# Order of the first seven steps in a four-layer graph attention kernel: a one-head step in third place

## The chip, the cores and the metric

The kernel runs on one core of a Trainium2 chip. The metric is the time of one execution on the device in microseconds (us), lower is better. A core has five engines that each work through a queue of their own: TensorE (PE in the profile; PEld is its loading of weights), VectorE (DVE), ScalarE (ACT), GpSimd (POOL), and SyncE (SP), which here only issues DMAs.

## The reference

Sixteen batches of 1024 nodes with 256 features go through four graph attention layers, one after the other, with a residual connection. The mask is one 1024x1024 adjacency matrix. Per layer:

```
h = relu(layernorm(x))
q = h @ W                              # per head: 4 heads of 64, or 1 head of 256
e = leaky_relu(q @ a_src + (q @ a_dst).T)      # 1024 x 1024 per head
p = softmax(where(adj > 0, e, -inf))
x = x + elu(p @ q)                     # relu in the last layer
```

Layers 0 and 2 have four heads, layers 1 and 3 have one. All arithmetic is in 32-bit floats.

## The kernel before

A *step* is one layer of one batch: 64 steps, `(batch, layer)`. Four batches are in flight at a time (streams 0 to 3), and `order_of_steps` gives the order in which their steps are taken, as a list of streams in `turns`. A step needs the step before it of the same stream to be finished.

A step has three phases.

- *Preparation* (`preparation`, a list of 21 pieces). `stats` takes bn_stats on VectorE, `combine` and `combine_end` make scale and shift of them (on GpSimd; on VectorE, with only the power on GpSimd, in step 0 and in the last step). `normalise` writes relu of the normalised rows on ScalarE. `transpose` turns them: in steps 0, 1 and the last by TensorE, with a copy on ScalarE; elsewhere by `split` (ScalarE), a DMA transpose (SP queue) and `merge` (ScalarE). `project` multiplies by the layer's weights on TensorE, its result `whx` is copied by ScalarE and scaled by GpSimd. `factors` and `rows` make the row factors, which go out to memory (`grow`) and come back broadcast over all partitions (`fetch`, tile `gs`), to be copied to PSUM by `broadcast` (tile `g`, two buffers). In step 0's first head and in the last step (`direct`) TensorE broadcasts instead.
- *Weights and aggregation*. `weights` makes one tile of attention weights, 128 x 1024, by one VectorE instruction (L455): the larger of row factor and column factor, times the mask. A four-head step has 32 such tiles, a one-head step 8. They have 18 buffers. `aggregate` sums them over `whx` on TensorE (L472): eight groups for a four-head step (`h`, `i0`), eight row blocks for a one-head step; ScalarE copies each group's result to `y` (L487).
- *Finishing* (`finish`): the division by the sum (`divide`), the elu (its exponential on ScalarE, L525) and the residual addition, on VectorE and GpSimd. In the third step from the end the finishing is done on VectorE as a chain of its own (`early`, `late`, `begin`, `end`), with the last step's statistics in it, since that step follows in the same stream with only one other step between.

The order within an engine is the order in which the Python code emits (`manual_schedule`). The main loop goes over steps and groups `k`: it aggregates a group, emits what finishing has at `k`, then the preparation pieces due, then further weight tiles, up to 6 (four heads) or 3 (one head) more. When a preparation piece is due is told by tables of 21 times in units of a group, eight to a step: `kind` chooses a table for a step and `start` the group from which it counts. Step 1 uses `FIRST`, step 2 uses `SOON`, the last one `LAST`. `slack(n)` says that the next step has one head.

Of the kernel before, what the change touches and what calls it, by code (L numbers as in the profile page):

```python
# [32 lines left out]
ALU = mybir.AluOpType  # L33
# [14 lines left out]

FOUR = (-8, -8, -5, 0, 1, 0, 3, 5, 5, 5, 5, 1, 4, 5, 5, 5, 5, 6, 8, 8, 10)
SHORT = (-4, -4, -4, 0, 1, 0, 3, 5, 5, 5, 5, 1, 4, 5, 5, 5, 5, 6, 8, 8, 10)
NEXT = (-4, -4, -4, 1, 3, 2, 5, 8, 8, 8, 8, 4, 7, 8, 8, 8, 8, 9, 10, 10, 12)
ONE = (2, 2, 2, 3, 4, 3, 5, 7, 7, 7, 7, 4, 7, 8, 8, 8, 8, 8, 11, 11, 12)
SOON = (0, 0, 0, 1, 2, 1, 3, 4, 4, 5, 5, 2, 5, 6, 6, 7, 7, 7, 8, 8, 10)
FIRST = (-4, -4, -4, -2, -0.9, -1, -1, -0.8, -0.8, -0.8, -0.8, 0, 0, 1, 1, 1, 1, 1, 2, 2, 4)
TIGHT = (4, 4, 4, 5, 6, 5, 7, 8, 8, 8, 8, 6, 8, 9, 9, 9, 9, 9, 10, 10, 12)
LAST = (0, 0, 0, 1, 3, 2.8, 2.8, 4, 4, 4, 4, 4, 4, 4, 4, 4, 4, 4, 5, 5, 5)
LATE = (0, 0, 0, 1, 2, 1, 3, 4, 4, 4, 4, 2, 4, 5, 5, 5, 5, 5, 6, 6, 8)


LAYERS = [
    (4, 0.2, 0, 0),
    (1, 0.2, 0, 0),
    (4, 0.2, 128, 1),
    (1, 0.01, 0, 1),
]
# [3 lines left out]
def kernel(ctx: ExitStack, tc: tile.TileContext, x, adj, ws, avs, out):  # L71
    nc = tc.nc
# [37 lines left out]

    L = len(LAYERS)
    steps = order_of_steps(B, L)
    xs = {}
    state = [dict() for _ in steps]

    def bank(*shape):
        t = ps.tile([P, 512], F32, name="bank")
        n = math.prod(shape)
        if len(shape) == 1:
            return t[:, 0:n]  # L120
        names = "abc"[:len(shape)]
        return t[:, 0:n].rearrange(f"p ({' '.join(names)}) -> p {' '.join(names)}",
                                   **dict(zip(names, shape)))
# [151 lines left out]
    def preparation(n):  # L275

        b, l = steps[n]
# [4 lines left out]
        def stats(half):  # L282
            if half == 0:
                st["bn"] = small.tile([P, C, 6], F32, name="bn")
            bn = st["bn"]
            for c in range(half * HALF, (half + 1) * HALF):
                nc.vector.bn_stats(bn[:, c, :], xs[b][:, c, :])  # L287
            q = slice(half * HALF, (half + 1) * HALF)
            if n == len(steps) - 1:
                combine(q, nc.vector)  # L290
            elif n == 0:
                if half == 1:
                    combine_end(slice(0, HALF), nc.vector)
                combine(q, nc.vector)
            elif H == 1:

                combine(q, nc.gpsimd)
                combine_end(q, nc.gpsimd)
# [26 lines left out]
        def combine_end(q, engine):  # L325
            rstd, shift = (st[i][:, q] for i in ("rstd", "shift"))
            engine.tensor_tensor(shift, shift, rstd, op=ALU.mult)
            engine.tensor_scalar(shift, shift, -0.5, None, op0=ALU.mult)  # L328
# [25 lines left out]
                st["turned", half].rearrange("p s n i -> p (n i) s"), AF.Copy)  # L354

        def transpose(half, k):
            if 1 < n < len(steps) - 1:

                (merge if k else split)(half)
                return  # L360
            if k == 0:
                st["hT", half] = prep.tile([P, K, HALF * P], F32, name="rows", bufs=HBUFS)
            pt = bank(HALF, P)
            for q in range(HALF):
                nc.tensor.transpose(pt[:, q, :], st["xn", half][:, k, q, :], ident)
            nc.scalar.activation(st["hT", half][:, k, :], pt.rearrange("p q i -> p (q i)"),
                                 AF.Copy)
# [28 lines left out]

        def rows():

            if n == len(steps) - 1:
                return  # L400
            pt = bank(P)[0:C * H]
            nc.tensor.transpose(pt, st["gcol"].rearrange("p c h -> p (c h)"), ident)  # L402
            gT = small.tile([C * H, P], F32, name="gT", bufs=2)
            nc.scalar.activation(gT, pt, AF.Copy)
            st["grow"] = dram.tile([H, C, P], F32, name="grow")
            nc.sync.dma_start(out=st["grow"].rearrange("h c i -> c h i"), in_=gT)
# [5 lines left out]


        out += [factors, rows, lambda: fetch_heads(n + 1), lambda: None]
        if n == len(steps) - 1:
            st["stats"], st["combined"] = stats, lambda half: combine_end(
                slice(half * HALF, (half + 1) * HALF), nc.vector)
            out[0:3] = [lambda: None] * 3
        return [(at, piece) for at, piece in zip(agenda_of[n], out, strict=True)]

    def direct(n, h):

        return h == 0 and n in (0, len(steps) - 1)

    def fetch(n, h):

# [16 lines left out]
    def weights(n, h, jc):  # L443


        parts = 2 if n == len(steps) - 1 else 1
        if parts > 1 and jc:
            return
        js = range(C) if parts > 1 else (jc,)
        for j in js:  # L450
            state[n]["w", h, j] = work.tile([P, N], F32, name="w", bufs=WBUFS)
        for i in range(parts):
            s = slice(i * N // parts, (i + 1) * N // parts)
            for j in js:
                nc.vector.scalar_tensor_tensor(  # L455
                    state[n]["w", h, j][:, s], state[n]["g", h][:, s],
                    state[n]["rcol"][:, j, h:h + 1],
                    masks[LAYERS[steps[n][1]][3]][:, j, s], op0=ALU.max, op1=ALU.mult)
# [30 lines left out]
    def slack(n):  # L489

        return LAYERS[steps[n + 1][1]][0] == 1

    def finish(n):

        b, l = steps[n]
# [27 lines left out]
        def exponential(half):  # L523
            if l < L - 1:
                nc.scalar.activation(st["e", half], st["e", half], AF.Exp)  # L525
# [19 lines left out]
            if half == 1 and b + STREAMS < B:  # L545
                load(b + STREAMS)

        if n == len(steps) - 3:

            def early(half):  # L550
                xh, yh, r = views(half)
                rb = r[:, :, None].to_broadcast([P, HALF * H, D])
                e = st["e", half] = prep.tile([P, HALF * H, D], F32, name="rows", bufs=HBUFS)
                nc.vector.scalar_tensor_tensor(e, yh, 0.0, rb, op0=ALU.min, op1=ALU.mult)  # L554
                if half == 0:
                    exponential(half)
                nc.vector.tensor_tensor(yh, yh, rb, op=ALU.mult)

            def late(half):
                xh, yh, r = views(half)  # L560
                e = st["e", half]
                nc.vector.scalar_tensor_tensor(e, e, -1.0, yh, op0=ALU.add, op1=ALU.max)
                nc.vector.tensor_add(xh, xh, e)

            def begin():
                divide()
                early(0)
                late(0)
                state[-1]["stats"](0)
                early(1)  # L570
                state[-1]["combined"](0)

            def end():
                late(1)
                state[-1]["stats"](1)
                state[-1]["combined"](1)

            return [(-1, begin), (1, lambda: exponential(1)), (1, end)]


        at = (0, 0, 0, 0, 1, 1, 1) if slack(n) and H > 1 else (0, 0, 1, 1, 2, 2, 3)
# [31 lines left out]
    def fetch_heads(below=0):  # L613

        done["rows"] = max(done["rows"], below)
        while done["gs"] < min(done["g"] + 2 * C, len(tiles)):
            n, h, _ = tiles[done["gs"]]
            if n >= done["rows"]:
                break
            fetch(n, h)  # L620
            done["gs"] += C
# [23 lines left out]
    for n, (b, l) in enumerate(steps):  # L645

        free = -99
        if b % STREAMS in last:
            over = last[b % STREAMS] + 1
            free = 8 * over + (8 if l == 0 else 2 if LAYERS[steps[over][1]][0] == 1 else 4)  # L650
        last[b % STREAMS] = n
        start = 8 * (n - 2)
        kind = ONE if LAYERS[l][0] == 1 else SOON if n < 3 else FOUR
        if kind is FOUR and free > start + kind[0]:
            kind = SHORT if slack(n - 2) else NEXT
        if kind is ONE and free > start + kind[0]:
            kind = TIGHT
        if free > start + kind[0]:
            kind = LATE
            start = max(free, agenda_of[-1][0] + 5, start - LATE[7])  # L660
        if n == len(steps) - 1:
            kind, start = LAST, 8 * (n - 1)
        agenda_of.append([start + k for k in kind] if n > 1 else FIRST)
        if n > 2:


            assert agenda_of[n][7] >= 8 * (n - 2)
            assert agenda_of[n][3] >= agenda_of[n - 1][12]
# [76 lines left out]
def order_of_steps(B, L):  # L745

    depth = B // STREAMS * L  # L750
    one = [[(k // L * STREAMS + s, k % L) for k in range(depth)] for s in range(STREAMS)]
    turns = [0, 1, 2, 0, 3, 1, 2] + [0, 3, 1, 0, 2, 1, 3, 2] * (depth // 2 - 1) + [3]
    return [one[s].pop(0) for s in turns]


# [22 lines left out]
```

## Time and profile before

| | us |
|---|---|
| median of 3 runs | 2445.25 |
| their range | 2444.63 to 2452.23 |
| profiled execution, its own time | 2449.74 |
| its span from first to last instruction | 2448.0 |
| busy: TensorE | 2394.8 (98%) |
| busy: VectorE | 2040.0 (83%) |
| busy: ScalarE | 1480.0 (60%) |
| busy: GpSimd | 1073.7 (44%) |

The profile is of one execution. A group of it collects the instructions of one line and form; behind the busy time stands the time that the engine was idle just before them, and what ended it. A timeline lists start, duration, engine, line, operation and count, with such idle time in brackets. Matmuls are pipelined, so a busy TensorE need not be at its peak.

Where the first seven steps end in this execution (by the last aggregation): step 1 at about 135 us, the third step, (2,0), at 180, and the seventh, (2,1), at 327.3.

### The profile page before, as it was taken

The numbers are of one execution on the slowest core, as the hardware profiler recorded it, in microseconds if no ns is written. First come the engines' busy times: TensorE is split into PE (matmuls) and PEld (weight loads), VectorE is DVE, ScalarE is ACT, GpSimd is POOL, SyncE is SP. The second block draws the span as 40 slices with busy tenths as digits, with TensorE's granted clock in tenths as the row PEclk, the third lists the DMA queues.
The fourth block names the chain that finished last, engine by engine and source line by source line (L and its number), as shares of the span: only waits on it lengthen the run. The fifth ranks groups of instructions, "written<-read, shape, count | busy, mean of one in ns | idle before, by whom it ended". The sixth has DMA issues, their size and how long they took to land.

```text
span 2448.0 us, 86681 instructions
## 1 busy us (share of the span) xinstructions
PE 2394.8 (98%) x39177; PEld 2153.2 (88%) x39177; DVE 2040.0 (83%) x2141; ACT 1480.0 (60%) x2505; POOL 1073.7 (44%) x1350
## 2 busy tenths in 40 slices
PE   7999999999999999999999999999999999999999
PEld 5888899899888888898998888888988998988987
DVE  8988588898888988887988888888889888888794
ACT  5465676565666656765656765566655577656542
POOL 3345455433345454544433554543443345545331
PEclk9999999999999999999999999999999999999999
DMA  5322233243333222323433322224334323223220
GB/s 182 83 53 63 45 79 67 66 114 92 85 96 79 72 63 52 74 71 96 114 89 88 80 62 71 64 50 108 75 93 114 95 48 80 68 65 76 75 54 35
DMA packets 292220, 191.84 MB, mean 78 GB/s; under 512 B 261778, under 2 KB 264586, under 8 KB 289930
## 3 DMA queue, kind: packets, MB, share of 16 engines
q1 hardware_dynamic: 291840, 186.29, 30.6%
q8 instruction: 307, 5.03, 0.9%
q14 instruction: 63, 0.52, 0.1%
q10 hardware_dynamic: 10, 0.00, 0.0%
HBM read 104.87 MB, written 17.43 MB: 50 GB/s over the span
## 4 chain that ended last, share of the span: by engine, by line
PE 82%; ACT 7%; DMA 5%; DVE 4%; issue 2%; POOL 0%; SPq 0%; DVEq 0%; ACTq 0%
PE bank L472 64%; PE bank L376 17%; DVE w L455 2%; DMA gs<-grow 2%; ACT rows L334 2%; DMA grow<-gT 2%; ACT g L441 1%; ACT rows L343 1%; ACT rows L525 1%; ACT rows L351 1%; ACT y L487 1%; DVE bn L287 1%; DMA rows<-rows 0%; PE bank L402 0%; ACT whx L378 0%
## 5 line engine op out<-in xcount | busy, mean ns | idle before, releaser
L472 PE MATMUL bank<-whx,w 128*64 128x65 f32 x36864 | 1898.0, 240 | 17.9 <-DVE w L455 9.3
L472 PEld LDWEIGHTS bank<-whx,w 128*64 128x64 f32 x36864 | 1745.7, 144 | 173.9 <-ACT whx L378 21.8
L455 DVE SCALAR_TENSOR_TENSOR w<-g,rcol,mask 128x1024 f32<-128x1024 f32 (+1 forms) x1288 | 1540.2, 1270 | 204.0 <-PE bank L472 165.2
L388 POOL TENSOR_TENSOR whx<-whx 128x1024 f32<-128x1024 f32 x128 | 244.5, 1910 | 819.1 <-ACT whx L386 819.1
L487 ACT ACTIVATE y<-bank 128x260 f32<-128x260 f32 (+1 forms) x504 | 192.1, 381 | 567.7 <-PE bank L472 567.7
L376 PE MATMUL bank<-wx,rows 128*128 128x264 f32 (+1 forms) x2048 | 484.8, 390 | 15.4 <-ACT y L487 11.8
L376 PEld LDWEIGHTS bank<-wx,rows 128*128 128x128 f32 x2048 | 380.9, 190 | 90.9 <-ACT y L487 17.9
L519 POOL TENSOR_TENSOR y<-y,r 128x1024 f32<-128x1024 f32 x124 | 259.0, 2098 | 222.0 <-DVE rows L518 188.4
L334 ACT ACTIVATE rows<-x,shift,rstd 128x256 f32<-128x256 f32 x512 | 265.2, 591 | 66.7 <-POOL shift L328 62.2
L378 ACT ACTIVATE whx<-bank 128x264 f32<-128x264 f32 (+1 forms) x512 | 193.7, 388 | 184.9 <-PE bank L376 184.6
L532 POOL TENSOR_TENSOR x<-x,rows 128x1024 f32<-128x1024 f32 x94 | 222.4, 2365 | 177.9 <-DVE rows L531 177.9
L351 ACT ACTIVATE rows<-rows 128x2048 uint16<-128x2048 uint16 x122 | 261.6, 2144 | 22.7 <-DMA rows<-rows 22.6
L343 ACT ACTIVATE rows<-rows 128x2048 uint16<-128x2048 uint16 x122 | 233.3, 1912 | 3.9
L531 DVE SCALAR_TENSOR_TENSOR rows<-rows,y 128x1024 f32<-128x1024 f32 x94 | 186.6, 1986 | 42.8 <-ACT rows L525 39.1
L287 DVE BATCH_NORM_STATS2 bn<-x 128x6 f32<-128x256 f32 x512 | 175.8, 412 | 34.5 <-POOL x L532 31.1
L441 ACT ACTIVATE g<-gs 128x1024 f32<-128x1024 f32 x158 | 161.8, 1024 | 67.1 <-DMA gs<-grow 55.9
L322 POOL TENSOR_TENSOR rstd<-rstd,neghalf 128x4 f32<-128x4 f32 (+1 forms) x97 | 121.3, 1251 | 41.1 <-DVE shift L323 33.8
L525 ACT ACTIVATE rows<-rows 128x1024 f32<-128x1024 f32 x96 | 100.7, 1048 | 4.2 <-DVE rows L554 4.2
L508 DVE RECIPROCAL r<-y 128x32 f32<-128x32 f32 (+1 forms) x63 | 17.4, 277 | 100.9 <-ACT y L487 100.9
L518 DVE SCALAR_TENSOR_TENSOR rows<-y,r 128x1024 f32<-128x1024 f32 x58 | 70.2, 1251 | 1.1
L386 ACT ACTIVATE whx<-whx,nbias 128x16 f32<-128x16 f32 (+1 forms) x128 | 40.4, 316 | 4.2
L384 ACT ACTIVATE rcol<-whx,rbias 128x16 f32<-128x16 f32 (+1 forms) x128 | 40.0, 313 | 4.2
(82 smaller groups left out, 461.9 us busy)
## 6 DMA issues: line engine op xcount, KB each, us to landing
gs<-grow SPq DMA_DIRECT2D x158, 512.0 KB
x<-in_x SPq DMA_DIRECT2D x15, 1024.0 KB
out<-x SPq DMA_DIRECT2D x30, 512.0 KB
w<-in_adj SPq DMA_DIRECT2D x8, 512.0 KB
rows<-rows SPq DMA_TRANSPOSE x122
x<-in_x SPq DMA_DIRECT2D x2, 512.0 KB
wx<-in_L_gnn_W SPq DMA_DIRECT2D x8, 128.0 KB
out<-x SPq DMA_DIRECT2D x8, 128.0 KB
```

The source lines that it names most:

```text
L287: nc.vector.bn_stats(bn[:, c, :], xs[b][:, c, :])
L334: nc.scalar.activation(xn[:, :, q, :], xs[b][:, c, :].rearrange("p (k i) -> p k i", k=K), AF.Relu, bias=st["shift"][:, c:c + 1], scale=st[ ...
L343: nc.scalar.activation(bits, xn.rearrange("p (n s) -> p s n", s=2), AF.Copy)
L351: nc.scalar.activation(st["hT", half].rearrange("p k i -> p (k i)").bitcast(U16).rearrange("p (n s) -> p n s", s=2), st["turned", half].re ...
L376: nc.tensor.matmul(pw, lhsT=st["hT", half][:, k, q * P:(q + 1) * P], rhs=wx[l][:, k, :], start=(k == 0), stop=(k == K - 1))
L378: nc.scalar.activation(st["whx"][:, c, :], pw, AF.Copy)
L388: nc.gpsimd.tensor_tensor(wh[:, :, :, 0:D], wh[:, :, :, 0:D], wh[:, :, :, D:D + 1].to_broadcast([P, HALF, H, D]), op=ALU.mult)
L455: nc.vector.scalar_tensor_tensor(state[n]["w", h, j][:, s], state[n]["g", h][:, s], state[n]["rcol"][:, j, h:h + 1], masks[LAYERS[steps[n] ...
L472: nc.tensor.matmul(acc[o % P:o % P + cols, q, :], lhsT=st["w", h, jc][:, o:o + cols], rhs=st["whx"][:, jc, h * (D + 1):(h + 1) * (D + 1)], ...
L487: nc.scalar.activation(st["y"][:, i0:i0 + per, h, :], acc, AF.Copy)
L519: nc.gpsimd.tensor_tensor(yh, yh, rb, op=ALU.mult)
L532: nc.gpsimd.tensor_add(xh, xh, e)
```

## The change

In the list of turns the third step becomes stream 0's one-head layer 1, and the two four-head steps of streams 2 and 3 come fourth and sixth:

```
before: (0,0) (1,0) (2,0) (0,1) (3,0) (1,1) (2,1) ...
after:  (0,0) (1,0) (0,1) (2,0) (1,1) (3,0) (2,1) ...
```

From the seventh step on the order is as before. The third step (n = 2) is treated as the last step is (`rush`): statistics combined on VectorE, transposes on TensorE, `direct` broadcast of its row factors, weights in halves; its preparation is placed by a new table `THIRD`, within step 1. Step 0 is finished by the chain on VectorE, save one multiplication on GpSimd; the chain is cut into `begin`, `middle` and `end`, `middle` and `end` at group 1 of step 1. The fourth step (n = 3) gets a new table `FOURTH`, counted from group 8 (the start of step 1), so its statistics come after group 4 of step 0 and its projections at the end of step 0 and after step 1's first group. `SOON` goes.

```diff
 FOUR = (-8, -8, -5, 0, 1, 0, 3, 5, 5, 5, 5, 1, 4, 5, 5, 5, 5, 6, 8, 8, 10)
 SHORT = (-4, -4, -4, 0, 1, 0, 3, 5, 5, 5, 5, 1, 4, 5, 5, 5, 5, 6, 8, 8, 10)
 NEXT = (-4, -4, -4, 1, 3, 2, 5, 8, 8, 8, 8, 4, 7, 8, 8, 8, 8, 9, 10, 10, 12)
 ONE = (2, 2, 2, 3, 4, 3, 5, 7, 7, 7, 7, 4, 7, 8, 8, 8, 8, 8, 11, 11, 12)
-SOON = (0, 0, 0, 1, 2, 1, 3, 4, 4, 5, 5, 2, 5, 6, 6, 7, 7, 7, 8, 8, 10)
 FIRST = (-4, -4, -4, -2, -0.9, -1, -1, -0.8, -0.8, -0.8, -0.8, 0, 0, 1, 1, 1, 1, 1, 2, 2, 4)
 TIGHT = (4, 4, 4, 5, 6, 5, 7, 8, 8, 8, 8, 6, 8, 9, 9, 9, 9, 9, 10, 10, 12)
+THIRD = (1, 1, 1, 1, 3, 1.8, 1.8, 1.9, 1.9, 1.9, 1.9, 3, 3, 3, 3, 3, 3, 3, 5, 5, 5)
+FOURTH = (-4, -4, -4, -3, -2, -3, -1, -1, -1, -1, -1, -2, 0, 0, 0, 0, 0, 0, 0, 0, 7)
 LAST = (0, 0, 0, 1, 3, 2.8, 2.8, 4, 4, 4, 4, 4, 4, 4, 4, 4, 4, 4, 5, 5, 5)
 LATE = (0, 0, 0, 1, 2, 1, 3, 4, 4, 4, 4, 2, 4, 5, 5, 5, 5, 5, 6, 6, 8)
...
     steps = order_of_steps(B, L)
     xs = {}
     state = [dict() for _ in steps]
+    rush = (2, len(steps) - 1)
     def bank(*shape):
         t = ps.tile([P, 512], F32, name="bank")
...
             for c in range(half * HALF, (half + 1) * HALF):
                 nc.vector.bn_stats(bn[:, c, :], xs[b][:, c, :])
             q = slice(half * HALF, (half + 1) * HALF)
-            if n == len(steps) - 1:
+            if n in rush:
                 combine(q, nc.vector)
             elif n == 0:
                 if half == 1:
...
                 st["turned", half].rearrange("p s n i -> p (n i) s"), AF.Copy)
         def transpose(half, k):
-            if 1 < n < len(steps) - 1:
+            if n > 1 and n not in rush:
                 (merge if k else split)(half)
                 return
...
         def rows():
-            if n == len(steps) - 1:
+            if n in rush:
                 return
             pt = bank(P)[0:C * H]
             nc.tensor.transpose(pt, st["gcol"].rearrange("p c h -> p (c h)"), ident)
...
         out += [factors, rows, lambda: fetch_heads(n + 1), lambda: None]
-        if n == len(steps) - 1:
+        if n in rush:
             st["stats"], st["combined"] = stats, lambda half: combine_end(
                 slice(half * HALF, (half + 1) * HALF), nc.vector)
             out[0:3] = [lambda: None] * 3
...
     def direct(n, h):
-        return h == 0 and n in (0, len(steps) - 1)
+        return h == 0 and (n == 0 or n in rush)
     def fetch(n, h):
...
     def weights(n, h, jc):
-        parts = 2 if n == len(steps) - 1 else 1
+        parts = 2 if n in rush else 1
         if parts > 1 and jc:
             return
         js = range(C) if parts > 1 else (jc,)
...
             if half == 1 and b + STREAMS < B:
                 load(b + STREAMS)
-        if n == len(steps) - 3:
+        if n + 2 in rush:
+            after = state[n + 2]
             def early(half):
                 xh, yh, r = views(half)
                 rb = r[:, :, None].to_broadcast([P, HALF * H, D])
                 e = st["e", half] = prep.tile([P, HALF * H, D], F32, name="rows", bufs=HBUFS)
                 nc.vector.scalar_tensor_tensor(e, yh, 0.0, rb, op0=ALU.min, op1=ALU.mult)
-                if half == 0:
-                    exponential(half)
-                nc.vector.tensor_tensor(yh, yh, rb, op=ALU.mult)
+                (nc.vector if n else nc.gpsimd).tensor_tensor(yh, yh, rb, op=ALU.mult)
             def late(half):
                 xh, yh, r = views(half)
...
             def begin():
                 divide()
                 early(0)
+            def middle():
+                exponential(0)
                 late(0)
-                state[-1]["stats"](0)
+                after["stats"](0)
                 early(1)
-                state[-1]["combined"](0)
+                after["combined"](0)
             def end():
+                exponential(1)
                 late(1)
-                state[-1]["stats"](1)
-                state[-1]["combined"](1)
-
-            return [(-1, begin), (1, lambda: exponential(1)), (1, end)]
+                after["stats"](1)
+                after["combined"](1)
+            return [(-1, begin), (-1 if n else 1, middle), (1, end)]
         at = (0, 0, 0, 0, 1, 1, 1) if slack(n) and H > 1 else (0, 0, 1, 1, 2, 2, 3)
...
             free = 8 * over + (8 if l == 0 else 2 if LAYERS[steps[over][1]][0] == 1 else 4)
         last[b % STREAMS] = n
         start = 8 * (n - 2)
-        kind = ONE if LAYERS[l][0] == 1 else SOON if n < 3 else FOUR
+        kind = ONE if LAYERS[l][0] == 1 else FOUR
         if kind is FOUR and free > start + kind[0]:
             kind = SHORT if slack(n - 2) else NEXT
         if kind is ONE and free > start + kind[0]:
...
         if free > start + kind[0]:
             kind = LATE
             start = max(free, agenda_of[-1][0] + 5, start - LATE[7])
-        if n == len(steps) - 1:
-            kind, start = LAST, 8 * (n - 1)
+        if n == 3:
+            kind, start = FOURTH, 8
+        if n in rush:
+            kind, start = THIRD if n == 2 else LAST, 8 * (n - 1)
         agenda_of.append([start + k for k in kind] if n > 1 else FIRST)
-        if n > 2:
+        if n > 3:
             assert agenda_of[n][7] >= 8 * (n - 2)
...
     depth = B // STREAMS * L
     one = [[(k // L * STREAMS + s, k % L) for k in range(depth)] for s in range(STREAMS)]
-    turns = [0, 1, 2, 0, 3, 1, 2] + [0, 3, 1, 0, 2, 1, 3, 2] * (depth // 2 - 1) + [3]
+    turns = [0, 1, 0, 2, 1, 3, 2] + [0, 3, 1, 0, 2, 1, 3, 2] * (depth // 2 - 1) + [3]
     return [one[s].pop(0) for s in turns]
```

## The prediction

> **What bounds the kernel now.** I read the page first, then the timelines of VectorE, TensorE and ScalarE up to 345 us, because the diff moves work only there. All later steps keep their order.
>
> From the page (share of the span; then count | busy us, mean ns | idle before):
>
> ```profile
> PE 2394.8 (98%) x39177; PEld 2153.2 (88%) x39177; DVE 2040.0 (83%) x2141; ACT 1480.0 (60%) x2505; POOL 1073.7 (44%) x1350
> ...
> L472 PE MATMUL bank<-whx,w 128*64 128x65 f32 x36864 | 1898.0, 240 | 17.9 <-DVE w L455 9.3
> ...
> L455 DVE SCALAR_TENSOR_TENSOR w<-g,rcol,mask 128x1024 f32<-128x1024 f32 (+1 forms) x1288 | 1540.2, 1270 | 204.0 <-PE bank L472 165.2
> ...
> L334 ACT ACTIVATE rows<-x,shift,rstd 128x256 f32<-128x256 f32 x512 | 265.2, 591 | 66.7 <-POOL shift L328 62.2
> ...
> L351 ACT ACTIVATE rows<-rows 128x2048 uint16<-128x2048 uint16 x122 | 261.6, 2144 | 22.7 <-DMA rows<-rows 22.6
> L343 ACT ACTIVATE rows<-rows 128x2048 uint16<-128x2048 uint16 x122 | 233.3, 1912 | 3.9
> ```
>
> TensorE is busy nearly all the time; a group of a four-head step takes 3.79 us back to back (the timeline has three in 11.36), a row block of a one-head step 3.53 us (three in 10.59), a projection 7.35 us. So a four-head step needs 8 x 3.79 + 7.35 + 0.27 = 38 us of TensorE, a one-head step 8 x 3.53 + 7.35 + 0.27 = 36. VectorE needs 32 weight instructions for a four-head step and 8 for a one-head step, at a pitch of 1.194 us (47.75 / 40 below): 38.2 us, and about 9 us of finishing and statistics on top, against 9.6 and some 6. A four-head step is thus bound by VectorE, a one-head step by TensorE. The start has three four-head steps in a row. VectorE's timeline (start us, us, engine, line, out<-in, count):
>
> ```profile
> 47.87 47.75 DVE L455 SCALAR_TENSOR_TENSOR w<-g,rcol,mask 128x1024 f32<-128x1024 f32 x40
> 95.53 0.35 DVE L508 RECIPROCAL r<-y 128x32 f32<-128x32 f32 x1
> ...
> 98.35 2.48 DVE L455 SCALAR_TENSOR_TENSOR w<-g,rcol,mask 128x1024 f32<-128x1024 f32 x2
> ...
> 107.94 1.23 DVE L531 SCALAR_TENSOR_TENSOR rows<-rows,y 128x1024 f32<-128x1024 f32 x1
> ...
> 112.64 7.23 DVE L455 SCALAR_TENSOR_TENSOR w<-g,rcol,mask 128x1024 f32<-128x1024 f32 x6
> ...
> 122.40 19.15 DVE L455 SCALAR_TENSOR_TENSOR w<-g,rcol,mask 128x1024 f32<-128x1024 f32 x16
> ```
>
> It runs without a hole, so it is the bound there. TensorE's timeline shows the price:
>
> ```profile
> 116.35 0.34 PE L472 MATMUL bank<-whx,w 128*64 128x65 f32 x4 [0.66 <-DVE w L455]
> 117.54 0.34 PE L472 MATMUL bank<-whx,w 128*64 128x65 f32 x4 [0.85 <-DVE w L455]
> ...
> 183.72 14.07 PE L472 MATMUL bank<-whx,w 128*128 128x257 f32 x64
> ```
>
> From 108 to 135 us TensorE takes four matmuls per weight tile and waits for the next (releaser L455). The last row is step 3's one-head work: four blocks in 14.07, without a wait. From 44.4 us (first aggregation) to 327.3 (end of the seventh step) TensorE's work is 32 x 3.79 + 24 x 3.53 + 3.65 + 6 x 7.35 + set-up of layers 1 to 3 (8.1) + rows (1.9) + transposes (1.1) = 265 us in 283: **18 us are lost there**, all that a better order could win.
>
> **What the Trainium skill says.** "Perfetto Trace Analysis", section Sequencer Loop: an engine instruction waits for its semaphores in its engine's queue, read in program order; so an instruction held up holds all behind it. The trace agrees: a group that TensorE ended at 143.99 us had its y copied at 147.07 only, behind a normalise and a split on ScalarE, and TensorE waited 0.70 us for that copy. "TensorE: Matmul & The Clock Gate", section What's actually happening: after an idle window of some 3.4 us the array runs at half clock for about as long. The trace agrees (PE, PEld, DVE, ACT, POOL busy, then clock granted):
>
> ```profile
> 33.00:36.70 3.70, 0.04 (x1) 0.00 (x0) 3.59 (x4) 3.32 (x5) 0.00 (x0) 0.76 0.27 82
> 36.70:39.60 2.90, 2.75 (x8) 1.48 (x8) 2.90 (x4) 2.88 (x7) 0.00 (x0) 0.50 0.74 263
> ```
>
> After 3.7 idle us the clock is 0.50, and the next 16 projection matmuls take 4.87 us in place of 3.75: 1.1 us for such a hole.
>
> **The change, part by part.** Following the planner's loop gives each engine's new order; the durations are those of before.
>
> *Order.* Stream 0's layer 1 becomes step 2, (2,0) step 3, (1,1) step 4, (3,0) step 5; from step 6 on all is as before. VectorE gets a one-head step after two four-head steps, not three.
>
> *Fourth step's preparation (n = 3).* Its bn_stats stand on VectorE behind step 0's 32 weight tiles. Those start at 35.7; without step 2's bn_stats at 45.3 they end at 73.9, the statistics (2.7) at 76.6. GpSimd's combination takes 4.2 (48.04 to 52.23 in this trace): 80.9. Then ScalarE, one after the other: normalise 2.08, split 1.91, y 0.37, normalise 2.08, split 1.91, y 0.37, g 1.02, merge 2.15 = 11.9 us, to **92.8**. The same chain in the trace of before:
>
> ```profile
> 124.84 2.08 ACT L334 ACTIVATE rows<-x,shift,rstd 128x256 f32<-128x256 f32 x4 [3.91 <-POOL shift L328]
> 126.95 1.91 ACT L343 ACTIVATE rows<-rows 128x2048 uint16<-128x2048 uint16 x1
> ...
> 134.17 2.13 ACT L351 ACTIVATE rows<-rows 128x2048 uint16<-128x2048 uint16 x1
> ```
>
> Split's end to merge's start leaves 5.3 us for the DMA transpose, issued from SP; here 5.6 us lie between, so I cost it at nothing; when late, it adds its excess (no landing is shown; waits of 0.4 and 1.4 us at 355 and 430 bound it). On SP the two transposes stand behind step 1's four gs loads, the last waiting for a buffer until about 76: no cost.
>
> TensorE has finished step 0's last group at 82.6 (step 0's fillers are gone) and now holds projections 0 to 3 of step 3 in front of step 1's first group. It **waits 10 us**, colder afterwards: projections to 97.5 (3.75 and 1.1), group (0,0) to 101.4, y, second merge on ScalarE to 104, projections 4 to 7 to 107.7, factors and rows to 109.8, group (0,1) to 113.7, its y to 114.1.
>
> *The chain.* finish(0) puts `exponential(0)` on ScalarE only after that y (piece `middle`, k = 1). VectorE comes to it earlier: 76.6 + 16 x 1.194 = 95.7, divide 0.35, early 1.22, two tiles 2.4: 99.7. `late(0)` then waits until 115.2. **VectorE stands 15 us**, with step 1's other 14 tiles behind it, and TensorE behind those. Then late 2.5, statistics 1.4, combination 1.1, early 1.2, `combine_end` 0.4 (121.8), exponential 1.05 and GpSimd's multiplication, late 2.5, statistics and combination 2.5, GpSimd's power, end: 130. That is 15 us, against 16.9 for the same chain of the last step, which has two more multiplications (1.25 each):
>
> ```profile
> 2381.12 1.23 DVE L562 SCALAR_TENSOR_TENSOR rows<-rows,y 128x1024 f32<-128x1024 f32 x1
> ...
> 2386.03 0.16 DVE L323 TENSOR_TENSOR shift<-bn 128x4 f32<-128x4 f32 x1
> ...
> 2394.88 0.16 DVE L327 TENSOR_TENSOR shift<-shift,rstd 128x4 f32<-128x4 f32 x1 [1.05 <-POOL rstd L322]
> ...
> 2409.32 10.62 DVE L455 SCALAR_TENSOR_TENSOR w<-g,rcol,mask 128x512 f32<-128x512 f32 x16 [14.07 <-PE g L438]
> ```
>
> The power is a visible 1.05 us hole there. "Unbroken" is relative: two exponentials and two powers stay outside VectorE. ScalarE's second exponential waits for the second early (121.2), and behind it stand step 1's last g and step 2's first normalise: cost inside the sum. The tiles follow: 14 x 1.194, 146.9.
>
> TensorE meanwhile: (1,0) to 118.3; step 2's transposes for normalise (125.5), projections to 130.8 (1 us more if cold), (1,1) 134.6, second transposes and projections 142, (2,0) and (2,1) 149.8, eight g transposes 150.9, (3,0) and (3,1) **159** (159.5 with half the cold cost). The last row above says what step 2's weights need: 16 halves, 10.6 us; the first eight are there at 156.2, in time.
>
> *Taken away and added for the one-head step.* Two DMA transposes with their splits and merges, grow, one gs load, one g copy, GpSimd's small operations go; 16 transposes (2.1 us) and eight g transposes (1.0) on TensorE come, 0.27 of rows goes: +2.8 us, in the sum. VectorE gets 18 small operations of 0.16 (in the chain).
>
> *Sum.* In the first two steps' stretch TensorE's work is 86.6 us (16 groups, 18.4 of projections, the small pieces), from 44.4 to 159.5: 28.5 us lost. From there it has 181 us more to do for the other five steps, and VectorE, one-head step in hand, is ahead: 159.5 + 181 = 340.5, and some 0.5 to 1 for the small waits that before shows there too. Against 327.3: **+13.5 us**. Profiled execution: 2449.74 (span 2448.0, 1.7 around it), so 2463; it stands 4.5 above the median of the runs, 2445.25, so **2459** for the median.
>
> *At nothing.* The agendas of steps 4 to 7 shift by a piece or two, under TensorE's unbroken rows after 180; if not covered, up to 3.4 us, as at 242 to 246 (four waits of 0.85), or as much less. The last step's pieces come out in the old order, so its end is as before. GpSimd's multiplication in place of VectorE's 1.25: it must only be ready before the exponential; uncovered, 2 us.
>
> **The rivals.** *R1, faster:* the exponential is not late. If the chain starts at 99.7, the weights bind again: 99.7 + 15 + 14 tiles = 131.4, then two groups, 139 to 141; 140 + 181 = 321 at the seventh step, 6 us less, 2439; with the 3.4 us of waits at 242 to 246 gone too, 2435.5. From a delay of 15 us of `late(0)` to none the end moves by 20, so the sign turns at a delay of about 5. For it: the stretch of three four-head steps goes, and 18 us are there to be had. Against: ScalarE's order, whose rows above are all measured. *R2, a wash:* the statistics run some 6 us earlier or pieces overlap more: half the delay, +3 to +4, 2449. *R3, worse:* transposes late, three cold holes instead of one, or steps 3 to 5 fall behind on VectorE: 5 to 9 us more, up to 2468. *R4:* the change doesn't take effect (chain no longer bound by order) is excluded: the turns are a fixed list.
>
> **How the numbers follow.** A measurement of this kernel tells about 0.3% (7.3 us) from no change. Forecast 0.63, own range 2453 to 2466; R3 0.08; R2 0.14, all but 0.01 within 7.3 us; R1 0.15, a third of it within. Slower 0.72, same 0.18, faster 0.10. The range from 2441 to 2470 leaves out most of R1 and the tail of R3.
>
> **What would show it.** Right: a hole of about 10 us on TensorE near 83 us ended by ScalarE's merge; a VectorE wait of some 15 us near 100 ended by ScalarE's exponential; step 2's one-head rows from about 159; the seventh step ending near 341. Wrong: no VectorE wait above 5 us near 100 (then R1), or the seventh step before 327.

## The result, and the profile after

| | before | after |
|---|---|---|
| median, us | 2446.68 (4 runs) | 2476.19 (4 runs) |
| range, us | 2444.63 to 2452.23 | 2472.44 to 2483.82 |
| ratio | | 1.0121 [1.009, 1.0152] |
| profiled execution (span), us | 2449.74 (2448.0) | 2483.82 (2482.0) |
| first aggregation to the end of the seventh step, us | 44.43 to 327.3: 282.9 | 44.40 to 355.3: 310.9 |

The change makes the kernel slower by 29.5 us (medians). The two profiled executions lie 34.1 us apart; 28 of these are lost before the seventh step ends, where 13.5 were forecast. The other 6 come behind it and are not in a second profile of the changed kernel (see Open). The new lines stand four further down: L459 makes weights, L476 aggregates, L380 projects, L338 normalises, L347 splits, L355 merges.

The groups of the page (count | busy us, mean ns of one | idle time before them, and what ended most of it):

```profile
L476 PE MATMUL bank<-whx,w 128*64 128x65 f32 x36864 | 1891.0, 240 | 14.2 <-issue 13.6
...
L459 DVE SCALAR_TENSOR_TENSOR w<-g,rcol,mask 128x1024 f32<-128x1024 f32 (+1 forms) x1296 | 1540.4, 1260 | 198.8 <-PE bank L476 172.0
...
L380 PE MATMUL bank<-wx,rows 128*128 128x264 f32 (+1 forms) x2048 | 492.6, 395 | 36.0 <-ACT rows L355 25.3
```

In the first row the waits for a weight tile, 9.3 us before, are no longer what ended most idle time, and up to the end of the seventh step none is left: that part of the change works. (Time that the profile calls "issue" is idle time in which the engine waited for nothing that the profile shows.) The third row is the price: 36 us of idle time in front of projections, 25.3 of it ended by a merge. TensorE's timeline (start, duration, engine, line, operation, count; in brackets the idle time before and what ended it) says where:

```profile
92.39 5.72 PE L380 MATMUL bank<-wx,rows 128*128 128x264 f32 x16 [9.79 <-ACT rows L355]
...
125.69 2.81 PE L369 MATMUL bank<-ident,rows 128*128 128x128 f32 x8 [6.86 <-ACT rows L338]
128.33 4.76 PE L380 MATMUL bank<-wx,rows 128*128 128x258 f32 x16
...
140.43 5.44 PE L380 MATMUL bank<-wx,rows 128*128 128x258 f32 x16 [0.25 <-ACT rows L370]
...
202.20 5.36 PE L380 MATMUL bank<-wx,rows 128*128 128x258 f32 x16 [12.09 <-ACT rows L355]
```

The hole before 92.4 is the forecast one, the last is not in the forecast. VectorE's timeline, first the forecast wait:

```profile
115.75 1.23 DVE L565 SCALAR_TENSOR_TENSOR rows<-rows,y 128x1024 f32<-128x1024 f32 x1 [16.20 <-ACT rows L529]
...
131.30 16.77 DVE L459 SCALAR_TENSOR_TENSOR w<-g,rcol,mask 128x1024 f32<-128x1024 f32 x14
154.60 17.78 DVE L459 SCALAR_TENSOR_TENSOR w<-g,rcol,mask 128x512 f32<-128x512 f32 x22 [6.54 <-PE g L442]
172.30 0.34 DVE L512 RECIPROCAL r<-y 128x32 f32<-128x32 f32 x1
...
188.05 1.41 DVE L291 BATCH_NORM_STATS2 bn<-x 128x6 f32<-128x256 f32 x4 [0.91 <-POOL x L536]
```

and ScalarE's:

```profile
162.16 0.39 ACT L491 ACTIVATE y<-bank 128x260 f32<-128x260 f32 x1 [3.34 <-PE bank L476]
...
191.55 2.07 ACT L338 ACTIVATE rows<-x,shift,rstd 128x256 f32<-128x256 f32 x4 [14.79 <-POOL shift L332]
...
200.01 2.14 ACT L355 ACTIVATE rows<-rows 128x2048 uint16<-128x2048 uint16 x1
```

The last three rows of VectorE and the three of ScalarE belong to one chain, from step 1's last y to step 4's first projection. Step 4 is (1,1), so its statistics need step 1, (1,0), to be finished. That y is copied at 162.16. The division by its sum starts at 172.30, because 16 half tiles of step 2, held until 154.60 by the g of TensorE, and six tiles of step 3 stand ahead of it on VectorE. Elu, two residual additions on GpSimd and the statistics end at 189.4. GpSimd's combination, normalise, split, DMA transpose and merge follow, and the projection starts at 202.20: 40 us after the y. In the kernel before, the same way had 74 us (ScalarE's and TensorE's rows of that trace), and the projection starts without a wait:

```profile
136.20 0.38 ACT L487 ACTIVATE y<-bank 128x260 f32<-128x260 f32 x1
...
210.36 3.65 PE L376 MATMUL bank<-wx,rows 128*128 128x258 f32 x16
```

After the change TensorE has one thing to do beside that, step 2's eight row blocks, until 190.1. The projections of step 4 then stand in its queue ahead of step 3's first group, whose weights are ready. The windows show what it did (us: length of the window; PE, PEld, DVE, ACT, POOL busy; then the clock granted to TensorE, the DMA share and GB/s):

```profile
93.00:98.00 5.00, 5.00 (x16) 3.78 (x14) 4.97 (x6) 1.17 (x3) 0.00 (x0) 0.67 0.01 3
...
190.00:202.00 12.00, 0.11 (x1) 0.00 (x0) 3.03 (x3) 10.38 (x13) 7.73 (x24) 0.72 0.34 62
...
208.00:355.30 147.30, 147.30 (x2458) 134.06 (x2455) 119.59 (x125) 93.91 (x159) 76.24 (x98) 1.00 0.28 65
```

TensorE idles for 12 us, and from 208 on it is busy without a break.

### The profile page after: what moved, and what is told of

Same layout as the page of the kernel before. It is cut to its first block, busy times and chain, and to the rows that moved or that the text cites. A ratio compares the mean times of both kernels' runs of the same rounds, so it can differ in the third digit from the quotient of the medians.

```text
span 2482.0 us, 86695 instructions
## 1 busy us (share of the span) xinstructions
PE 2401.2 (97%) x39200; PEld 2158.7 (87%) x39200; DVE 2050.9 (83%) x2173; ACT 1473.7 (59%) x2503; POOL 1060.2 (43%) x1326
## 4 chain that ended last, share of the span: by engine, by line
PE 85%; ACT 6%; DMA 3%; DVE 3%; issue 2%; POOL 1%; SPq 0%; DVEq 0%; ACTq 0%
PE bank L476 66%; PE bank L380 18%; ACT rows L338 2%; DMA gs<-grow 2%; DVE w L459 2%; DMA grow<-gT 1%; ACT rows L347 1%; ACT rows L529 1%; ACT g L445 1%; ACT y L491 0%; DVE bn L291 0%; ACT rows L355 0%; PE bank L406 0%; POOL x L536 0%; DMA x<-in_x 0%
## 5 line engine op out<-in xcount | busy, mean ns | idle before, releaser
L476 PE MATMUL bank<-whx,w 128*64 128x65 f32 x36864 | 1891.0, 240 | 14.2 <-issue 13.6
L476 PEld LDWEIGHTS bank<-whx,w 128*64 128x64 f32 x36864 | 1741.3, 144 | 168.4 <-issue 26.9
L459 DVE SCALAR_TENSOR_TENSOR w<-g,rcol,mask 128x1024 f32<-128x1024 f32 (+1 forms) x1296 | 1540.4, 1260 | 198.8 <-PE bank L476 172.0
L380 PE MATMUL bank<-wx,rows 128*128 128x264 f32 (+1 forms) x2048 | 492.6, 395 | 36.0 <-ACT rows L355 25.3
L380 PEld LDWEIGHTS bank<-wx,rows 128*128 128x128 f32 x2048 | 387.7, 194 | 113.6 <-ACT rows L355 32.9
L338 ACT ACTIVATE rows<-x,shift,rstd 128x256 f32<-128x256 f32 x512 | 264.5, 588 | 79.1 <-POOL shift L332 72.8
L355 ACT ACTIVATE rows<-rows 128x2048 uint16<-128x2048 uint16 x120 | 257.3, 2144 | 20.4 <-DMA rows<-rows 20.2
L347 ACT ACTIVATE rows<-rows 128x2048 uint16<-128x2048 uint16 x120 | 229.3, 1911 | 3.8
L512 DVE RECIPROCAL r<-y 128x32 f32<-128x32 f32 (+1 forms) x63 | 17.3, 275 | 124.2 <-ACT y L491 124.2
L390 ACT ACTIVATE whx<-whx,nbias 128x4 f32<-128x4 f32 (+1 forms) x128 | 40.3, 315 | 4.2
L388 ACT ACTIVATE rcol<-whx,rbias 128x4 f32<-128x4 f32 (+1 forms) x128 | 39.9, 312 | 4.3
```

Of the source, the lines that this page charges most:

```text
L338: nc.scalar.activation(xn[:, :, q, :], xs[b][:, c, :].rearrange("p (k i) -> p k i", k=K), AF.Relu, bias=st["shift"][:, c:c + 1], scale=st[ ...
L347: nc.scalar.activation(bits, xn.rearrange("p (n s) -> p s n", s=2), AF.Copy)
L355: nc.scalar.activation(st["hT", half].rearrange("p k i -> p (k i)").bitcast(U16).rearrange("p (n s) -> p n s", s=2), st["turned", half].re ...
L380: nc.tensor.matmul(pw, lhsT=st["hT", half][:, k, q * P:(q + 1) * P], rhs=wx[l][:, k, :], start=(k == 0), stop=(k == K - 1))
L459: nc.vector.scalar_tensor_tensor(state[n]["w", h, j][:, s], state[n]["g", h][:, s], state[n]["rcol"][:, j, h:h + 1], masks[LAYERS[steps[n] ...
L476: nc.tensor.matmul(acc[o % P:o % P + cols, q, :], lhsT=st["w", h, jc][:, o:o + cols], rhs=st["whx"][:, jc, h * (D + 1):(h + 1) * (D + 1)], ...
```

## Experiments

All are measured by two numbers: the ratio to the kernel before, run beside it on the same chip, with its interval, and the stretch from the first aggregation to the end of the seventh step in the profile (282.9 us before). Executions start up to 2.4 us apart, so the stretch is safer than the end alone, and times of two runs are compared from the first aggregation of each. Each stretch is that of one execution; the two kernels with two profiles agree with themselves within 0.6 us.

| kernel | ratio | stretch, us |
|---|---|---|
| before again (b0_before) | | 282.4 |
| after again (after_again) | 1.0137 [1.0116, 1.0158] | 311.5 |
| e1_exp_early | 1.0108 [1.0091, 1.0125] | 302.0 |
| e2_step4_late | 1.017 [1.0155, 1.0185] | 319.6 |
| e5_step3_early | 1.0083 [1.0062, 1.0104] | 294.8 |
| e6_both | 1.0115 [1.0094, 1.0136] | 302.7 |
| e7_hold | 1.0047 [1.0032, 1.0062] | 288.3 |
| e8_third_late | 1.0051 [1.0034, 1.0069] | 294.5 |
| e9_three | 1.0027 [1.0014, 1.004] | 286.8 |
| e10_no_chain | 1.0036 [1.0025, 1.0047] | 290.3 |
| e11_chain_later | 1.0035 [1.0024, 1.0046] | 286.2 |
| e12_best | 1.0036 [1.0022, 1.005] | 281.9 |

**The two unchanged kernels.**

> The kernel before, with its profile on the chip of the others: seventh step at about 327 us; what follows it to the last step's aggregation takes 2076 to 2082 us here as in the others, so that a difference of the times is one of the first seven steps.

> The changed kernel on the same chip as the three others, as the measure for them: ratio to before 1.012, seventh step at 355, all theories alike.

Both stretches are within 0.6 us of the first profiles: the 28 us are no accident of one execution.

**Is the late exponential the price?** In e1_exp_early the chain doesn't wait for step 1's first group; the rest stays.

```diff
 def begin():
     divide()
     early(0)
+    if n == 0:
+        exponential(0)
+        early(1)
+        exponential(1)
...
```

`middle` and `end` leave these three out for step 0.

> Step 0's two exponentials and the second early piece are issued at the start of the chain, ahead of step 1's first group; TensorE's 9.8 us hole near 83 us stays. Theory A (VectorE's 16.2 us wait near 99.5 is ScalarE's order, and it is what step 1's end hangs on): the wait falls to some 4 us (GpSimd's multiplication is there at 103), step 1 ends 8 to 12 us earlier, about 152, time 2464 to 2468. Rival B (TensorE's own holes set the end of step 1 and VectorE's wait is slack): no more than 3 us, 2473 to 2476.

The 16.2 us wait of VectorE falls to 3.0, now for GpSimd's multiplication. The stretch shrinks by 9 us, as theory A had it, and not by the 13 that VectorE won. The hole ahead of step 3's projections (9.74 us) and the one ahead of step 4's (12.18) are as in the changed kernel.

**Later projections for step 4.** e2_step4_late moves step 4's preparation behind step 3's third group.

```diff
+FIFTH = (2, 2, 2, 5, 6, 5, 7, 10, 10, 10, 10, 6, 8, 11, 11, 11, 11, 11, 12, 12, 13)
...
+        if n == 4:
+            kind = FIFTH
```

> Step 4's normalise, merges and projections are due two to four groups later, so step 3's first three groups stand ahead of its projections on TensorE; all else as after. Theory A2 (the 12.1 us hole at 190 to 202 is TensorE's order: groups whose tiles are ready stand behind projections that wait for GpSimd and ScalarE): the hole goes, and with it 1.6 us of cold clock, 12 to 14 us, time about 2463. Rival B2 (step 4's preparation is late for all that follows, so the wait is only put off to step 4's first block or to the next projections): under 4 us, 2472 or more.

It failed: 9 us longer. The 12 us hole is gone, but TensorE's timeline has others (lines one further down):

```profile
203.72 0.48 PE L477 MATMUL bank<-whx,w 128*64 128x65 f32 x4 [4.08 <-DVE w L460]
...
221.42 2.09 PE L381 MATMUL bank<-wx,rows 128*128 128x258 f32 x4 [7.39 <-ACT y L492]
```

and VectorE's the reason for more:

```profile
252.07 8.44 DVE L460 SCALAR_TENSOR_TENSOR w<-g,rcol,mask 128x1024 f32<-128x1024 f32 x7 [16.35 <-ACT g L446]
```

The pieces moved so far back now crowd ScalarE beside step 5's: y copies stand behind normalise and split, and step 4's row factors reach VectorE 16 us late.

**Step 3 prepared earlier.** e5_step3_early starts its statistics four groups earlier, so its projections spread between step 0's and step 1's groups.

```diff
-FOURTH = (-4, -4, -4, -3, -2, -3, -1, -1, -1, -1, -1, -2, 0, 0, 0, 0, 0, 0, 0, 0, 7)
+FOURTH = (-8, -8, -8, -7, -6, -7, -5, -4, -4, -3, -3, -6, -3, -2, -2, -1, -1, -1, 0, 0, 7)
```

> Step 3's preparation at the places that the third step's had before the change (statistics after step 0's first group, projections between groups 4 and 7 of step 0); the order of steps and the chain stay. Theory A1 (late statistics of step 3 make both the 9.8 us hole and, through ScalarE, VectorE's wait): both go, exponential at about 99, step 1 ends at 141 to 147, 15 to 20 us earlier; time 2457 to 2461. Rival B (the chain on VectorE itself is what costs, whatever stands ahead of it): under 8 us, above 2468.

One edit takes away the hole at 83 us and with it the wait for the exponential (VectorE's timeline):

```profile
101.47 1.23 DVE L565 SCALAR_TENSOR_TENSOR rows<-rows,y 128x1024 f32<-128x1024 f32 x1 [1.02 <-ACT rows L529]
```

The stretch shrinks by 16 us: the two forecast waits were one cause, the late preparation, and cost 16 us together. The hole at step 4 stays, 12.02 us, and moves forward to 187.45.

**Both.**

> The edits of e5_step3_early and e2_step4_late together. Theory A: the gains add, 27 to 33 us, seventh step at 322 to 328, time 2443 to 2449, no longer slower than before the change. Rival: they don't add, since step 4's statistics depend on the same VectorE queue: some 20 us, 2456.

The edits of e5 and e2 together give 302.7, 8 us worse than e5 alone: e2's move costs about as much here as the 9 us that it cost alone.

**Step 1 finished earlier.** e7_hold adds to e5 that no tile of step 3 is made ahead of step 1's finishing.

```diff
+                if n == 1:
+                    upto = min(upto, place[3, 0, 0])
```

> e5_step3_early, with step 3's first six tiles held back until step 2, so that step 1's divide follows step 2's weight halves on VectorE directly. Theory C (the 12 us hole before step 4's projections comes of a chain from step 1's last y to step 4's merge, 40 us long, that has only step 2's 28 us of TensorE to lie beside, and that starts 10 us late because VectorE has 16 halves and six tiles ahead of the divide): the chain starts 7 us sooner, the hole shrinks to 3 to 6 us, seventh step 6 to 9 us earlier than in e5_step3_early, ratio to before 1.005. Rival C2 (the 28 us of step 2 bind only through TensorE's order, or step 3's tiles then come late): no gain, or TensorE waits for step 3's tiles instead.

```profile
181.46 5.24 PE L380 MATMUL bank<-wx,rows 128*128 128x258 f32 x16 [5.30 <-ACT rows L355]
```

The hole falls from 12.0 to 5.3 us and the stretch by 6.5. So six tiles, 7 us of VectorE, ahead of the division were a part of the chain and all of it counted.

**Step 2's transposes later.** e8_third_late (e5, with THIRD's transposes at 2.8 and 2.9 in place of 1.8 and 1.9, so that a ready group stands ahead of them) was to fill the wait for normalise.

> e5_step3_early, with step 2's first transposes and projections one group later, behind the group (1,1) of step 1 that is ready. Theory D (after the statistics chain TensorE, cold after 7 us of waiting for step 2's normalise with a ready group behind it, is what sets step 1's end): step 1 ends 4 to 6 us earlier, seventh step likewise, ratio 1.006. Rival D2 (VectorE's 14 tiles after the chain set it): no change, since they are not touched.

It fills it and gains nothing. TensorE's timeline:

```profile
111.84 0.33 PE L369 MATMUL bank<-ident,rows 128*128 128x128 f32 x1 [3.27 <-ACT rows L338]
...
114.49 6.21 PE L380 MATMUL bank<-wx,rows 128*128 128x258 f32 x16
...
125.03 6.04 PE L380 MATMUL bank<-wx,rows 128*128 128x258 f32 x16
138.62 1.09 PE L442 MATMUL g<-ident,gcol 128*128 128x128 f32 x8
```

The wait of 7.01 us in e5 is 3.27 here, but the projections take 6.2 and 6.0 us in place of e5's 4.4 and 5.4, and g comes 92.3 us after the first aggregation in place of 92.9. Its median is 6 us lower than e5's all the same. The intervals of the two ratios overlap (1.0062 and 1.0069 are their near ends), so this may be chance; the profile doesn't show a reason.

**Together.** e9_three is e7 and e8, with step 5's statistics later (-5.5 in place of -8).

> The edits of e7_hold and e8_third_late together, and step 5's statistics behind step 4's on VectorE (2.7 us out of the chain). Theories C and D: 12 to 16 us less than e5_step3_early, seventh step at 325 to 329, ratio to before 1.000 to 1.003. If the new order has a gain in it beyond that of before, this is where it must begin to show; the rival that a one-head step in third place is too short a cover for any order gives 1.004 or more.

The stretch is 286.8, 1.5 below e7's; 3.7 us of the hole remain. The seventh step ends at 332.9, later than the 325 to 329 expected; the ratio is inside its range.

**What the chain is worth.** e10_no_chain is e9 with step 0 finished on GpSimd and step 2 turned by DMA transposes, as an ordinary step. The order of steps stays.

> e9_three with the chain on VectorE undone: step 0 finished and step 2 combined on GpSimd as in other steps, step 2 turned by DMA, its projections behind step 1's last group. Theory E (the chain holds VectorE for 20 us where its tiles bind, but without it the way from step 0's last y to step 2's projections is just as long): VectorE's tiles of step 1 end about 12 us sooner, TensorE then waits 8 to 15 us for step 2's merge; seventh step at 330 to 338, ratio 1.002 to 1.006. Rival E2 (VectorE's time in the chain is all of the loss): seventh step at 322 or earlier, ratio under 1.000.

The stretch is 3.5 us longer. VectorE gets step 1's tiles done at 122.5, which is 77.9 us after the first aggregation and not 87.9 as in e9, and then stands idle:

```profile
141.69 4.04 DVE L459 SCALAR_TENSOR_TENSOR w<-g,rcol,mask 128x512 f32<-128x512 f32 x6 [19.17 <-ACT g L445]
```

Step 2's tiles start 97.0 us after the first aggregation, in e9 93.5: later by 3.5, as the stretch is longer. Whichever way step 0 is finished, the way from its last y to step 2's row factors is about as long, and that way, not VectorE's time in the chain, seems to set the order's price. No run shortens it by much, so this is an inference from e9, e10 and e11.

**Chain later.** e11_chain_later is e9 with the exponentials first, the chain in one piece behind eight more tiles of step 1, and step 2's transposes and projections behind the groups of these tiles.

> e9_three with step 1's third head's eight tiles ahead of the rest of the chain, the exponentials before them, both halves of the chain in one piece, and step 2's transposes and projections behind that head's groups. Theory F (TensorE stands from 108 to 131 us with little to do, since the chain holds VectorE while only two heads' tiles are there): TensorE has two groups more beside the chain, step 1 ends 2 to 7 us earlier, seventh step at 326 to 331, ratio 1.000 to 1.002. Rival F2 (step 2's projections then come later by as much, and stand before the last head's groups): 332 or later, ratio 1.003 or more.

Counted from the first aggregation, g comes at 91.6 us, 0.7 earlier than in e9, and the stretch is 286.2, 0.6 below e9's. The ratio, 1.0035, misses the 1.000 to 1.002 expected. The hole at step 4 and its cold projection (3.67 and 6.35 us) are unchanged.

**Both ends.** e12_best is e11 with step 4's projections one group later, so that the first four stand behind step 3's first group; the rest of its preparation stays, but for the second merge:

```diff
+FIFTH = (2, 2, 2, 3, 4, 3, 5, 8, 8, 8, 8, 4, 8, 9, 9, 9, 9, 9, 11, 11, 12)
```

> e11_chain_later with step 4's first projections one group later, behind step 3's first group, its rows where they were. Theory C: the hole of 3.7 us before them and the cold clock after it (6.35 us in place of 3.75) go without anything taking their place, as VectorE has step 3's first two heads nearly done: seventh step at 324 to 326, the ratio to before 0.998 to 1.002; the new order's own gain is then at most 3 us. Rival C3 (as in e2_step4_late something else is late by as much: y copies, VectorE's divide, step 4's row factors): 329 to 332, ratio 1.003.

TensorE's timeline at step 4 (lines one further down):

```profile
177.98 3.75 PE L381 MATMUL bank<-wx,rows 128*128 128x258 f32 x16
...
189.11 1.14 PE L381 MATMUL bank<-wx,rows 128*128 128x258 f32 x4 [0.68 <-ACT y L492]
191.27 7.69 PE L477 MATMUL bank<-whx,w 128*64 128x65 f32 x256 [1.02 <-ACT whx L383]
```

The hole is gone and the projection is warm. The stretch is 281.9, as before the change; the ratio, 1.0036, is nevertheless nearer the rival's 1.003 (see Open). One group was enough where e2's three were too many.

No version was found that beats the kernel before. Of the 18 us that the prediction calls lost there, TensorE is idle for 12.3 (busy 270.6 of 282.9), 9.3 of them ended by a weight tile; the rest is work that took longer than it was counted. e12 has no wait for a weight tile in its stretch but 10.8 us of other idle time (busy 271.1 of 281.9): the new order spends nearly all that it wins. By the prediction's count of TensorE's work, with its 2.8 us for the one-head step, e12 loses 281.9 - 265 - 2.8 = 14 us. Seen are 7.1 us of idle TensorE between 118 and 137.5 (busy 12.44 of 19.5), while chain and transposes of step 2 are under way; 2.4 us of colder projections there (5.90 and 3.81 against 2 x 3.65); 1.7 us at step 4; and 1.68 us of "issue" at 109.85, in which TensorE waited for nothing that the profile shows. That is 13 of 14.

**Open.** The ratios say more than the stretches. e12's median is 8 us above that of before beside it (2451.2 and 2443.3) at an equal stretch, and of the other new orders most are 4 to 9 us further from before than their stretch. Part may be the yardstick: the two profiled executions of before, 2449.74 and 2450.09, lie 3.1 and 5.8 us above the medians of their runs, and e12's, 2449.88, lies 1.3 below its own. An equal stretch of these executions doesn't show an equal stretch of usual ones. Behind the seventh step the profiles show no difference between the orders: 2075 to 2083 us to the last aggregation (before 2081.7 and 2082.2), a spread as wide as what is to be explained. Only the changed kernel's first profile, its slowest run, has 2087.7; its second has 2075.1, and 7.8 of these 12.6 us are "issue" time of TensorE (17.3 and 9.5). Where a usual execution of before is shorter was not seen.

## Why the prediction was wrong in size

**Right.** Slower, by the mechanism named first, and in its place:

| step | forecast | measured |
|---|---|---|
| TensorE's hole ahead of step 3's projections | 10 us, to 92.8 | 9.79, to 92.39 |
| second merge and projections | from 104 | 104.51 |
| `late(0)` waits on VectorE | 15, to 115.2 | 16.20, to 115.75 |
| end of the chain | 130 | 131.3 |
| end of step 1's 14 tiles | 146.9 | 148.1 |
| last y of step 1 | 159 to 159.5 | 162.2 |
| seventh step ends | 340.5 to 341 | 355.3 |

**Mis-sized: the cold projections.** The sum had 1.1 us for one cold hole. Three projections of the stretch took 5.72, 4.76 and 5.44 us; with 3.75 for a warm one that is 4.7 us over. The sum had 1.1 for the first and, in its upper value, 0.5 for the second. The granted clock over these rows is 0.66, 0.78 and 0.68; time times clock gives 3.6 to 3.7 us, the warm time, so the clock is all of it. The price of 1.1 us had also left out the transposes that the hole stands before: in the trace of before the eight behind the hole took 2.79 us, the next eight, at 48.47, 1.09. Step 1 ended 2.7 to 3.2 us late, with the chain 1.3 late and this work; no run tells the two shares apart. The Trainium skill, "TensorE: Matmul & The Clock Gate", section What's actually happening, has the array at half clock after an idle window of about 3.4 us until a busy one of that length has passed. If half clock is all there is, a projection of 5.72 us was at half clock for 2 x (5.72 - 3.75) = 3.9 us (an estimate), one of e9's 6.35 for 5.2: near it for the first, longer for the second.

**The step that failed: "From there it has 181 us more to do ... VectorE, one-head step in hand, is ahead", and, put at nothing, "The agendas of steps 4 to 7 shift by a piece or two, under TensorE's unbroken rows after 180".** TensorE's rows are not unbroken there. Work without the hole took 355.3 - 162.2 - 12.1 - 1.6 = 179.4 us, 2 less than the 181 taken; the hole and its cold projection added 13.7. So: 13.5 forecast, + 2.9 at step 1, + 13.7, - 2 = 28. I counted work after 159 and asked VectorE's weights only whether they come in time. I didn't follow the preparation of step 4, which needs step 1's finishing. In the order before, (1,0) and (1,1) are second and sixth, with three steps between; now two lie between. The projections stand ahead of the last of these, so the cover falls from two steps (74 us from y to projection) to one: 28 us of row blocks against a chain of 40. The forecast delay of step 1 isn't the cause: in e5 its last y is copied 16.2 us earlier, counted from the first aggregation, and the hole is 12.02 us. In both, g of step 2 comes right ahead of step 1's last two groups, so that 16 half tiles and six more stand ahead of step 1's division. e7 (7 us off the chain, 6.7 off the hole) and e12 (one ready group ahead of the projections, no hole) show both ends of it.

**Rivals.** R1's condition, an exponential in time, was made true by e1 and e5. It gave 9 and 16 us, not the 20 that its slope from 15 us to none promised, and the sign never turned. R1 had step 1 over by 139 to 141; in e5, with `late(0)` at 101.5, TensorE starts step 1's last two groups only at 139.74. R1 put VectorE's tiles alone on the path and left out what stands between the groups on TensorE: step 2's transposes and projections, with 7 us of waiting for normalise and some 2.5 of colder work. R3 named three cold holes, or steps 3 to 5 falling behind on VectorE. Three holes came (9.79, 6.86 and 12.09 us), and the stretch is the right one; but what fell behind is step 4's preparation, of which VectorE's queue is a part, and R3's 5 to 9 us stand against 13.7. R2's half delay isn't in any run. R4 was rightly excluded.

## What to carry over

When steps change places, take each stream's chain from its last y through finishing, statistics, transposes to projection, and compare its length with what the in-order engine that it feeds has ready ahead of that projection: here one step of 28 us did not cover a chain of 40, and 74 us of the order before did. A sum of TensorE's work holds only while no such chain ends late. To mend such a hole, put one ready group ahead of the late piece and shorten what stands ahead of the chain's first instruction; pushing the whole preparation back moves the wait elsewhere.

## What was not expected of the hardware

Filling half of an idle stretch can leave its cost as it was. In e8 a ready group went into a 7.01 us hole, and the 16 projections behind the 3.27 us that were left took 6.2 us in place of 4.4, at a granted clock of 0.60 in place of 0.84. In e5 a part of the cost fell on the eight transposes ahead of them: 2.81 us, 1.09 for the same eight in e1, which had no hole there.

GpSimd and VectorE hold each other up in small operations. In the changed kernel, VectorE's product of 128 x 4 took 1.86 us in place of its usual 0.16 while GpSimd multiplied from 122.82 to 124.72:

```profile
122.87 1.86 DVE L331 TENSOR_TENSOR shift<-shift,rstd 128x4 f32<-128x4 f32 x1 [0.92 <-POOL rstd L326]
```

and GpSimd's power beside VectorE's `early` took 2.02 us, 1.01 alone. The Trainium skill, "GPSIMD Engine Reference", section Specifications, names the interface that the two share when a VectorE instruction has two inputs in SBUF; the traces agree. Both times came again in after_again, e5, e7 and e8; in e11, where GpSimd multiplies nothing beside it, the product took 0.16. It cost the chain 2.6 us (1.7 of the product, 0.9 of waiting for the power) of the 15.5 that it took.
